# A transformer block on one core: seven products for eight in the second projection of the gated layer's first token block

## The chip, the core and the metric

The kernel runs on one core of a Trainium2 chip, in float32. The time is the device time of one execution, in microseconds (us), and the median of several runs is given. The engines that matter here are PE (matrix products; weights are loaded beside them, PEld), DVE (elementwise work and reductions, reads PE's result banks), ACT (activation functions and copies, reads the banks too), POOL (elementwise work on the on-chip memory only) and SP (issues transfers).

## The reference

A block of three layers over `x` of 2 x 1024 tokens x 256: self-attention with 16 heads of 64, cross-attention to 154 context tokens, and a gated layer, each on a layer norm of `x` and added to `x`. The gated layer, to which the change belongs:

```python
h = _layernorm(x, ln3_g, ln3_b)
p = h @ ff_w1 + ff_b1
a, gate = (p[..., :D_FF], p[..., D_FF:])              # D_FF = 1024
h = a * jax.nn.gelu(gate, approximate=False) @ ff_w2 + ff_b2
return h + x
```

Below, u is `a * gelu(gate)`, 1024 features for each token; the first projection is the product with `ff_w1`, the second the one with `ff_w2` (1024 x 256).

## The kernel before

The attention stages come first and fill most of the span. The gated layer runs in one loop at the end, over slots k = 0 to 63. Its tokens come in four blocks ("pairs") of 512, two of each batch element; a block is two halves j = 0, 1 of 256 tokens, and a half two tiles of 128. A unit n is one block and one slice f of 128 features (f = 0 to 7), and takes two slots: `gate_first(n)` in the even slot, `gate_second(n)` in the odd one. So block 0 is in slots 0 to 15, block 1 in 16 to 31, and so on.

**The first projection** makes, for a unit, the four 128 x 256 results (value and gate for both halves) from seven products for eight, a scheme after Strassen and Winograd: combined weights (`weight_sums`, made on POOL during cross-attention) and combined tokens (`token_sums`, four POOL operations for a block, called in slot 8 for block 1). DVE adds the parts (L1058, L1060, L1074, L1077, L1086), ACT applies the gate's function, and POOL multiplies value by gate: L1079 for half 1 at the end of `gate_second`, L1088 for half 0 in `gate_last`, which is called from the next unit's `gate_first`. These two write u.

**The second projection** of a block is queued in `sums` when its last unit is closed (slot 16 for block 0, 32 for block 1), and every slot takes two products of 256 columns, or one group of four products of 128 columns, from it.

- Block 0 is not in `FAST`: `sum_slot` (L1204) makes the plain product, eight products of 256 columns for each of four token tiles, 32 in all; DVE adds the result to `x` (L1214) and a transfer writes it out.
- Blocks 1 to 3 are in `FAST`: `fast_sum` (L1174) makes, for each half, seven groups g = 0 to 6 of four products of 128 columns. They read u itself (g=0, 1), mixes of u (s1, s2, s4, and one in the place of a21) and combined weights. DVE adds each group to its quarter of `x` (L1188); the first group is copied by ACT (L1182) and added to three quarters by POOL (L1183).

The mixes of u are `quick_tokens`: four POOL operations of 128 x 128 for each half and each pair of feature slices, queued in `combos` by `gate_last` when an odd f is closed. The combined weights of `ff_w2` are `quick_weights`: four POOL operations of 128 x 512 (L1136 to L1139). Both write a tile of the pool `pt`, tag `pT`, which `hold_quick` takes. That pool has two buffers: one holds the gated layer's weights (`wf`), the other the ring of cross-attention's turned probabilities, last read by PE in slot 5. `hold_quick` and the weights stand in slot k = 2 * NF + 2 = 18, and each slot takes two operations off `combos`.

**The order** on every engine is that of the program, written by hand: nothing reorders it, and an engine that waits holds up all that is behind. Within a slot stand, in this order: `gate_first` or `gate_second`, `token_sums` where due, the sums, the operations of `combos`, then `run_work`, which in odd slots takes a step from `side`, and an entry of `later` (L324 on POOL, the bias added to `x`). From slot 7 on, `side` holds the layer norm of the second batch element, which blocks 2 and 3 need: for two tiles a step, first statistics (DVE, L240, L241), a step later the variance and its root (POOL, L246, L250), a step later the offset (DVE, L256) and the normalization (POOL, L271, twice), and a step later four transposes on PE (L284). ACT moves the result to `hT`.

Of the kernel before, what the change touches and what calls it, by code (L numbers as in the profile page):

```python
# [10 lines left out]
ALU = mybir.AluOpType  # L11
# [7 lines left out]
def tile_transformer_block(ctx: ExitStack, tc: tile.TileContext, a: dict, out: bass.AP):  # L19
# [32 lines left out]
    NF = DF // P  # L52
# [45 lines left out]
    for n in names:  # L98
        k = n_of[n]
# [67 lines left out]
    for n in names[2:]:  # L167
        own = rows[row_of[n] - n_cols:row_of[n] - n_cols + n_of[n], :]
# [161 lines left out]
    def norm_beside(kind, b):  # L330

        after = {"sa": None, "ca": "sa", "ff": "ca"}[kind]
        stats, deviation, normalize, turn = norm_pieces(kind, b)
        n = 1 if narrow(kind, b) else 2
        lag = {}
        for fns, first in ((turn, 3), (stats, 0), (deviation, 1), (normalize, 2)):
            for i, fn in enumerate(fns):  # L340
                t = i if fns is stats else 2 * i + 1
                lag.setdefault(first + t // n, []).append((fn, fns is turn))
        for k in range(NT // n + 3):
            tiles = tile_order(kind)[k * n:(k + 1) * n]
            needs = [(after, b, half, t) for half in range(NQ) for t in tiles if after]

            def step(fns=lag[k]):
                slow.extend(fn for fn, _ in fns if fn in stats)
                done = [fn() for fn, _ in fns if fn not in stats]
                return next((fn for fn in done if fn), None)  # L350

            side.append((any(turns for _, turns in lag[k]), needs, step))
        if not narrow(kind, b):
            side.append((False, (), lambda: add_biases(kind, b)))
# [130 lines left out]
    def out_order(kind):  # L485

        return [t for t in tile_order("ff" if kind == "ca" else "ca") if t % 2 == 0]
# [75 lines left out]
    def run(piece):  # L563
        done = piece()
        if done is not None:
            (adds if getattr(done, "adds", False) else stores).append(done)

    def flush(queue):
        for fn in queue:
            fn()  # L570
        queue.clear()

    def run_work(n, n_side, bank=None, n_sum=0):

        while n > 0 and work:
            n -= work[0].banks
            run(work.pop(0))  # L580
        for _ in range(min(n_side, len(side))):
            needs_bank, needs, fn = side[0]
            if needs_bank and not bank and n <= 0 or not added.issuperset(needs):
                break
            if needs_bank and not bank:
                n -= 1
            spare["bank"] = bank or mm_tile
            run(fn)
            side.pop(0)
        if not spare["turned"]:  # L590
            flush(slow)
        for i in range(min(max(n, 0) + n_sum, len(outs))):
            spare["out"] = mm_tile if i < n else sum_tile
            run(outs.pop(0))

    def out_pieces(kind, b, half, tiles):
        outs.extend(lambda t=t: out_piece(kind, b, half, t) for t in tiles)
# [136 lines left out]
    CG = [(t, min(TG, NT - t)) for t in range(0, NT, TG)]  # L734
# [149 lines left out]
    def cross_regroup(c):  # L884

        ui, n = divmod(c - len(CG) - (1 if c > CA - 6 else 2), len(CG))
        if n != 0 or not 0 <= ui < NU:
            return
        for a2 in range(2):
            for a4 in range(P // KB):  # L890
                half, e = divmod(a4, 2)
                own = slice(a4 * KB, (a4 + 1) * KB)
                src = slice((2 * half + a2) * KB, (2 * half + a2 + 1) * KB)
                blocks = pTc["ring"][src, ui % 3, :2 * NM].rearrange("p (m e) j q -> p m e (j q)", e=2)
                nc.sync.dma_start(
                    out=pTc["pairs"][own, a2].rearrange("p m j q -> p m (j q)"), in_=blocks[:, :, e])
# [46 lines left out]
    def cross_drain(c):  # L943

        n = c - 2
        if 0 <= n < CA:
            cross_turn(n)

    def cross_weigh(c):

        ui, n = divmod(c - 2 * len(CG) - 1, len(CG))
        if n == 0 and 0 <= ui < NU:
            for part in (1, 0) if pools else (0, 1):
                run(lambda: cross_values(ui, part))
            flush(stores)


    NPR = B * 2
    BT = S // 4
    FU = NPR * NF  # L960
    wsum, wh, ub, psum, pools = {}, {}, {}, {}, {}
# [50 lines left out]
    def token_sums(pair):  # L1012

        b, t0 = divmod(pair * 2 * BT, S)
        h = hT["ff", b]
        own = [[h[:, c, t0 + j * BT:t0 + (j + 1) * BT] for j in range(2)] for c in range(NC)]
        t = pp_.tile([P, 3, BT], F32, tag="P", name=f"hs{pair}")
        nc.gpsimd.tensor_tensor(t[:, 0, :], own[0][1], own[0][0], ALU.subtract)
        nc.gpsimd.tensor_tensor(t[:, 1, :], own[1][1], t[:, 0, :], ALU.subtract)
        nc.gpsimd.tensor_tensor(own[0][1], own[1][1], own[0][1], ALU.subtract)  # L1020
        nc.gpsimd.tensor_tensor(t[:, 2, :], own[1][0], t[:, 1, :], ALU.subtract)
        wh[pair] = {
            1: own[0][0], 2: own[1][0], 3: own[1][1], 4: t[:, 2, :],
            5: t[:, 0, :], 6: t[:, 1, :], 7: own[0][1],
        }
# [55 lines left out]
    def gate_last(n):  # L1081
# [6 lines left out]
        nc.gpsimd.tensor_tensor(ub[pair][0][:, f, :], own[:, 0, :], own[:, 3, :], ALU.mult)  # L1088
        if pair in FAST and f % 2:
            for j in (1, 0) if pair == NPR - 1 else (0, 1):  # L1090
                engine = nc.vector if n == FU - 1 and j else nc.gpsimd
                combos.extend(((pair, j), fn) for fn in quick_tokens(pair, j, f // 2, engine))
        if f == NF - 1 and pair in FAST:
            order = [(j, g) for j in range(2) for g in range(7)]
# [5 lines left out]
                (lambda i=i, e=e: sum_slot(pair, i, e), 1) for i in range(2 * TF) for e in range(NF))  # L1100

    sums, summed, quick, combos, mixed = [], {}, {}, [], {}
    FAST = range(1, NPR)
    NHF = NF // 2

    def hold_quick():
# [34 lines left out]

    def quick_tokens(pair, j, c, engine=nc.gpsimd):

        u, own = ub[pair][j], quick["u", (2 * pair + j) % 4]
        (a11, a12), (a21, a22) = (
            [u[:, 2 * c + h, e * P:(e + 1) * P] for h in range(2)] for e in range(2))
        s1, s2, s4 = (own[:, i, c, :] for i in range(3))
        tt = engine.tensor_tensor
        mixed[pair, j] = mixed.get((pair, j), 0) + 1
        return [  # L1150
            lambda: tt(s1, a21, a22, ALU.add),
            lambda: tt(s2, s1, a11, ALU.subtract),
            lambda: tt(a21, a11, a21, ALU.subtract),
            lambda: tt(s4, a12, s2, ALU.subtract),
        ]

    def fast_sum(pair, j, g):
# [63 lines left out]
    with tc.manual_schedule():  # L1221
# [11 lines left out]
        own = [ps_s.tile([P, 2, HB], F32, tag="s", name=f"first_{r}") for r in range(2)]  # L1233
# [186 lines left out]
        for k in range(2 * FU):  # L1420
            c = CA + k
            if k == 0:
                run_work(0, 0, n_sum=2)
            flush(adds)
            (gate_second if k % 2 else gate_first)(k // 2)
            flush(stores)
            flush(lates)
            if k == 2 * len(CG) + 1:
                norm_beside("ff", B - 1)
            cross_drain(c)  # L1430
            if k % 2:
                cross_weigh(c - 1 if k == len(CG) + 2 else c)
            cross_regroup(c)
            if k == len(CG) + 2:
                out_pieces("ca", B - 1, NQ - 1, out_order("ca"))
            if k % (2 * NF) == NF and k < 2 * FU - 2 * NF:
                token_sums(k // (2 * NF) + 1)
            n_left = 2
            while n_left > 0 and sums:
                fn, n = sums.pop(0)  # L1440
                n_left -= n
                run(fn)
            flush(stores)
            if k == 2 * NF + 2:
                hold_quick()
                combos[:0] = [(None, fn) for fn in quick_weights()]
            for _ in range(min(2, len(combos))):
                combos.pop(0)[1]()
            run_work(0 if k == 1 else 1 + k % 2, k % 2)
            if later and (k <= len(CG) + 2 or k > 2 * NF):  # L1450
                if k <= len(CG) + 2 or k % 2:
                    later.pop(0)()
# [39 lines left out]
```

## Time and profile before

| | us |
|---|---|
| median of 3 runs | 1076.43 (1075.42 to 1077.2) |
| profiled execution, span | 1075.6 |
| busy PE / DVE / POOL / ACT | 1062.3 / 882.6 / 774.7 / 645.4 |
| slots k = 0 to 63 and the last sums | from 903.13 to the end |

The page gives the profiled execution's span and no other time for it. In a row of the timeline stand the start, the duration, the engine, the line of the kernel, the operation with what it writes and reads, its shape, how many follow each other, and in brackets an idle time before it with what ended it. A product in float32 leaves two records on PE. The tiles `quick` hold the combined weights and the mixes, `u` and `kT` the two halves of block 0's u, `own` a unit's parts, `pf` and `pq` the second projection's banks.

### The profile page before, as it was taken

How to read it: one execution, taken by the hardware profiler on the slowest of the kernel's cores; microseconds unless marked ns; L12 is line 12 of the kernel's file. 1: busy time of each engine (PE TensorE's matmuls, PEld its weight loads, DVE VectorE, ACT ScalarE, POOL GpSimd, SP SyncE). 2: the span in 40 equal slices, each digit the busy share in tenths (PEclk: the TensorE clock that was granted, in tenths of full speed). 3: DMA queues.
4: the chain of work that ended last, by engine and by line, in shares of the span. 5: the costliest groups of instructions: out<-in, count | busy, mean ns of one | idle time of the engine just before them, and what ended most of it. 6: DMA issues, size and time to landing. Idle time of an engine off the chain costs nothing.

```text
span 1075.6 us, 46812 instructions
## 1 busy us (share of the span) xinstructions
PE 1062.3 (99%) x19300; PEld 701.7 (65%) x19300; DVE 882.6 (82%) x1321; ACT 645.4 (60%) x2068; POOL 774.7 (72%) x1652
## 2 busy tenths in 40 slices
PE   8999999999999999999999999999999999999998
PEld 6556556566565565676655655566766677788998
DVE  5799999998989989999989898968877887655554
ACT  5766766677666666666777676665565564342231
POOL 2677777777777777777777777776666876499884
PEclk9999999999999999999999999999999999999999
DMA  3222122112111121111111101025776545000000
GB/s 91 65 74 48 44 48 53 43 43 50 31 43 31 33 51 34 38 43 24 44 24 34 43 24 38 16 57 138 173 171 169 124 107 113 17 5 16 21 10 30
DMA packets 104726, 60.84 MB, mean 57 GB/s; under 512 B 32378, under 2 KB 95298, under 8 KB 104514
## 3 DMA queue, kind: packets, MB, share of 16 engines
q1 hardware_dynamic: 103138, 57.07, 22.3%
q8 instruction: 152, 2.49, 1.0%
q10 hardware_dynamic: 1376, 0.79, 0.2%
q14 instruction: 60, 0.49, 0.2%
HBM read 27.91 MB, written 2.10 MB: 28 GB/s over the span
## 4 chain that ended last, share of the span: by engine, by line
PE 87%; DVE 3%; DMA 3%; POOL 3%; SPq 2%; issue 1%; ACT 1%; POOLq 0%; DVEq 0%; ACTq 0%
PE po L550 19%; PE s L498 18%; PE py_sa L472 5%; PE py_ca L472 5%; PE pv_sa L398 5%; PE pk_sa L367 4%; PE pq_sa L367 4%; PE pq_ca L367 4%; PE poc L914 4%; PE pb L1035 4%; PE pq L1174 3%; PE pa L1035 2%; PE sc L834 2%; PE pc L1035 2%; DMA st<-st 2%; SPq L519 2%
## 5 line engine op out<-in xcount | busy, mean ns | idle before, releaser
L622 POOL TENSOR_SCALAR p<-p,rd,ee 128x512 f32<-128x512 f32 x512 | 390.3, 768 | 91.3 <-DVE rd L612 88.2
L509 ACT ACTIVATE p<-s,st 128x512 f32<-128x512 f32 x512 | 345.0, 686 | 173.1 <-DVE st L684 170.4
L684 DVE TENSOR_REDUCE st<-s 128x2 f32<-128x1024 f32 x256 | 308.3, 1205 | 58.9 <-issue 18.2
L647 DVE STREAM_TRANSPOSE pT<-p 128x1024 f32<-128x1024 f32 x256 | 302.7, 1218 | 2.2 <-POOL p L622 2.1
L498 PE MATMUL s<-k_sa,q_sa 64*32 64x512 f32 x4096 | 252.9, 591 | 2.9 <-ACT p L509 2.2
L550 PE MATMUL po<-pT,v_sa 64*32 64x256 f32 x8192 | 237.1, 376 | 0.9 <-DVE pT L647 0.9
L550 PEld LDWEIGHTS po<-pT,v_sa 64*32 64x32 f32 x8192 | 172.6, 106 | 76.5 <-issue 30.6
L498 PEld LDWEIGHTS s<-k_sa,q_sa 64*32 64x32 f32 x4096 | 79.5, 106 | 102.9 <-issue 56.2
L851 ACT ACTIVATE p<-sc,neg 128x154 f32<-128x154 f32 x256 | 96.1, 403 | 79.9 <-DVE rden L859 76.3
L862 POOL TENSOR_SCALAR p<-p,rden 128x154 f32<-128x154 f32 x256 | 96.8, 399 | 52.8 <-DVE rden L859 52.6
L509 ACT ACTIVATION_READ_ACCUMULATOR p<-s,st 128x1 f32 x512 | 103.9, 203 | 0.0
L527 POOL TENSOR_TENSOR dd<-st 128x8 f32<-128x8 f32 x128 | 25.6, 200 | 73.8 <-DMA st<-st 70.8
L398 PEld LDWEIGHTS pv_sa<-sa_wv,hT_ln 64*128 64x128 f32 x1024 | 58.5, 188 | 14.2 <-issue 6.7
L398 PE MATMUL pv_sa<-sa_wv,hT_ln 64*128 64x128 f32 x1024 | 61.7, 275 | 0.0
L367 PE MATMUL pq_ca<-hT_ln,ca_wq 64*64 64x512 f32 (+1 forms) x544 | 59.9, 590 | 0.7 <-DMA ca_wq<-in_L_xattn_ca_wq_dram 0.5
L472 PE MATMUL py_ca<-ca_wo,o_ca 128*128 128x256 f32 x256 | 60.2, 383 | 0.0
L472 PE MATMUL py_sa<-sa_wo,o_sa 128*128 128x256 f32 x256 | 59.7, 385 | 0.3 <-ACT v_sa L407 0.3
L840 DVE TENSOR_REDUCE neg<-sc 128x6 f32<-128x924 f32 (+1 forms) x48 | 47.8, 995 | 14.8 <-PE sc L834 14.8
L472 PEld LDWEIGHTS py_sa<-sa_wo,o_sa 128*128 128x128 f32 x256 | 47.3, 190 | 18.4 <-issue 6.9
L367 PE MATMUL pq_sa<-hT_ln,sa_wq 64*32 64x512 f32 (+1 forms) x976 | 56.9, 586 | 0.0
L367 PE MATMUL pk_sa<-hT_ln,sa_wk 64*32 64x512 f32 x960 | 56.1, 590 | 0.3 <-ACT q_sa L382 0.3
L851 ACT ACTIVATION_READ_ACCUMULATOR p<-sc,neg 128x1 f32 x256 | 56.1, 219 | 0.0
(145 smaller groups left out, 1462.3 us busy)
## 6 DMA issues: line engine op xcount, KB each, us to landing
wf<-pT_ca SPq DMA_DIRECT2D x128, 128.0 KB, 2.4
st<-st SPq DMA_DIRECT2D x512, 1.0 KB, 1.8
v_sa<-v_sa SPq DMA_DIRECT2D x32, 256.0 KB, 4.1
sa_wq<-in_L_xattn_sa_wq_dram SPq DMA_DIRECT2D x32, 128.0 KB, 3.4
sa_wk<-in_L_xattn_sa_wk_dram SPq DMA_DIRECT2D x32, 128.0 KB, 3.3
sa_wv<-in_L_xattn_sa_wv_dram SPq DMA_DIRECT2D x32, 128.0 KB, 3.6
ca_wq<-in_L_xattn_ca_wq_dram SPq DMA_DIRECT2D x32, 128.0 KB, 3.4
wf<-in_L_xattn_ff_w_dram SPq DMA_DIRECT2D x12, 256.0 KB
```

The source lines that it names most:

```text
L367: nc.tensor.matmul(pq[r][f:f + m, at:at + n], lhsT=wt[own, c, f:f + m], rhs=h[own, c, t0:t0 + n], start=(c == 0), stop=(c == NH - 1), tile ...
L398: nc.tensor.matmul(pv[r][:, i * P:(i + 1) * P], lhsT=h[own, c, i * P:(i + 1) * P], rhs=wt[own, c, :], start=(c == 0), stop=(c == NH - 1), ...
L472: nc.tensor.matmul(py[:, e * D:(e + 1) * D], lhsT=o[:, i, (t + e) * P:(t + e + 1) * P], rhs=wo[kind][:, g * HP + i, :], start=(i == 0), st ...
L498: nc.tensor.matmul(sc[a4 * KB:(a4 + 1) * KB, j, :], lhsT=q[r, c:c + KB], rhs=k[r, h * HB:(h + 1) * HB], start=True, stop=True, tile_positi ...
L509: nc.scalar.activation(pr[:, j, :], sc[:, j, :], AF.Exp, bias=st[:, 0, 0, i, j:j + 1], accum_out=st[:, 0, 1, i, j:j + 1],)
L550: nc.tensor.matmul(po[a2][d:d + KB, :QH // 2], lhsT=v[r, t, e, d:d + KB], rhs=pT[r, d // DH * NK + n, :], start=(t == 0 and e == 0), stop= ...
L622: nc.gpsimd.tensor_scalar(pr[:, j, :], pr[:, j, :], own["rd"][:, c:c + 1], own["ee"][:, 0, c:c + 1], op0=ALU.mult, op1=ALU.mult,)
L647: nc.vector.transpose(halves[h][:, :, c:c + KB], slots[p]["p"][i].rearrange("p j (n k) -> p (j n) k", k=KB))
L684: nc.vector.tensor_reduce(st[:, 0, 0, i, :], sc[i], AX.X, ALU.max, negate=True)
L851: nc.scalar.activation(pr_[:, j, i, :T], sc[:, j, i * T:(i + 1) * T], AF.Exp, bias=neg[:, j, i:i + 1], accum_out=den[:, j, i:i + 1],)
L862: nc.gpsimd.tensor_scalar(pr_[:, j, i, :T], pr_[:, j, i, :T], rden[:, j, i:i + 1], 1.0, op0=ALU.mult, op1=ALU.mult,)
L1035: nc.tensor.matmul(into[:, :BT], lhsT=lhs, rhs=wh[pair][i], start=first, stop=True, skip_group_check=True)
```

## The change

Block 0 goes into `FAST`: its second projection is made by `fast_sum`, from mixes. Its mixes are queued from slot 4 on. `hold_quick` and the four weight operations go from slot 18 to slot 6 (2 * len(CG), where CG has three entries). No operation is taken off `combos` before slot 6, three a slot from 6 to 17, and two from 18 on. `quick_tokens` looks up its tile when an operation runs, not when it is queued, since the tile isn't there in slot 4. For block 0 there are 32 mixes more on POOL, 56 products of 128 columns for 32 of 256 on PE, and per half one copy on ACT, one addition on POOL and six on DVE, for four additions on DVE in all.

```diff
-    FAST = range(1, NPR)
+    FAST = range(NPR)
...
     def quick_tokens(pair, j, c, engine=nc.gpsimd):
-        u, own = ub[pair][j], quick["u", (2 * pair + j) % 4]
+        u = ub[pair][j]
...
-        s1, s2, s4 = (own[:, i, c, :] for i in range(3))
         tt = engine.tensor_tensor
+
+        def s(i):
+            return quick["u", (2 * pair + j) % 4][:, (0, 1, None, 2)[i - 1], c, :]
+
         mixed[pair, j] = mixed.get((pair, j), 0) + 1
         return [
-            lambda: tt(s1, a21, a22, ALU.add),
-            lambda: tt(s2, s1, a11, ALU.subtract),
+            lambda: tt(s(1), a21, a22, ALU.add),
+            lambda: tt(s(2), s(1), a11, ALU.subtract),
             lambda: tt(a21, a11, a21, ALU.subtract),
-            lambda: tt(s4, a12, s2, ALU.subtract),
+            lambda: tt(s(4), a12, s(2), ALU.subtract),
         ]
...
-            if k == 2 * NF + 2:
+            if k == 2 * len(CG):
                 hold_quick()
                 combos[:0] = [(None, fn) for fn in quick_weights()]
-            for _ in range(min(2, len(combos))):
+            n_mix = 0 if k < 2 * len(CG) else 3 if k < 2 * NF + 2 else 2
+            for _ in range(min(n_mix, len(combos))):
                 combos.pop(0)[1]()
```

The lines of the changed kernel lie one to four lower from here on (L1136 keeps its number, the mixes are L1154 to L1157, `fast_sum`'s product is L1177).

## The prediction

> **What bounds the kernel now.** I read the page first, then the stretches of the last stage (the windows view), then the chain of waits, and last the timelines of POOL and PE around the change. The page's engine row and the head of its chain:
>
> ```profile
> PE 1062.3 (99%) x19300; PEld 701.7 (65%) x19300; DVE 882.6 (82%) x1321; ACT 645.4 (60%) x2068; POOL 774.7 (72%) x1652
> PE 87%; DVE 3%; DMA 3%; POOL 3%; SPq 2%; issue 1%; ACT 1%; POOLq 0%; DVEq 0%; ACTq 0%
> ```
>
> PE is the bound over the whole span, so products saved on PE should come off the end, as long as nothing else becomes late. The windows view says where something might (after the stretch's length: busy us of PE, PEld, DVE, ACT, POOL, then PE's granted clock):
>
> ```profile
> 933.33:950.54 17.21, 16.12 (x76) 12.71 (x75) 13.07 (x38) 7.50 (x17) 15.95 (x27) 1.00 0.00 1
> 950.54:985.30 34.76, 34.76 (x166) 30.61 (x166) 16.82 (x41) 11.33 (x25) 32.68 (x53) 1.00 0.04 12
> ```
>
> In the gated layer's loop, the first stretch holds slots k=9 to 17, the second the rest up to k=31. From 933 to 951 us POOL is busy 15.95 of 17.21 us, and that is the one stretch where PE has gaps (16.12 of 17.21). The chain of waits and PE's timeline tie the two together:
>
> ```profile
> 945.18 1.09 POOL xn_ln L271 x2
> 953.78 0.86 PE pf L1204 x4
> 987.46 0.89 PE pq L1174 x8
> ```
> ```profile
> 941.21 0.70 PE L1035 MATMUL pb<-hT_ln,wf 128*128 128x256 f32 x2 [0.74 <-DVE own L1058]
> ...
> 950.59 1.03 PE L1204 MATMUL pf<-wf,u 128*128 128x256 f32 x4
> 951.45 0.60 PE L284 MATMUL ph_ln<-ident,xn_ln 128*128 128x128 f32 x4
> 951.88 0.60 PE L1035 MATMUL pa<-hT_ln,wf 128*128 128x256 f32 x2
> ```
>
> The chain itself runs through POOL's normalization of the second batch (L271) at 945 us: here POOL, not PE, already sets the pace for a moment. So I price PE's saving first and then POOL's load.
>
> **PE's saving.** A product leaves two records. Two old products of 256 columns (x4) take 0.86 us in the chain, 0.43 each, as the gate's products of the same shape do; four new ones of 128 columns (x8) take 0.89. Block 0 now has 16 slots of two, 13.8 us; it will have 14 slots of four, 12.5 us. The saving is 1.3 us, not an eighth more than that, because the narrow products run a little longer per column. By itself it would give 1075.6 - 1.3 = 1074.3 us of span.
>
> **POOL's added load.** POOL executes in order. Its timeline, from the first slot that changes (k=6) onward:
>
> ```profile
> 926.85 0.73 POOL L1088 TENSOR_TENSOR u<-own 128x256 f32<-128x256 f32 x1 [5.59 <-DVE own L1086]
> 931.22 0.72 POOL L1079 TENSOR_TENSOR kT<-own 128x256 f32<-128x256 f32 x1 [3.64 <-ACT own L1078]
> ...
> 934.01 0.73 POOL L1018 TENSOR_TENSOR hs<-hT_ln 128x256 f32<-128x256 f32 x1
> ...
> 936.87 0.73 POOL L1079 TENSOR_TENSOR kT<-own 128x256 f32<-128x256 f32 x1
> 937.67 0.19 POOL L246 TENSOR_SCALAR var_ln<-mv_ln 128x2 f32<-128x2 f32 x1
> 937.95 0.71 POOL L250 TENSOR_TENSOR rstd_ln<-var_ln,power 128x2 f32<-128x2 f32 x1
> 938.63 0.73 POOL L1088 TENSOR_TENSOR u<-own 128x256 f32<-128x256 f32 x1
> ...
> 941.15 1.09 POOL L271 TENSOR_SCALAR xn_ln<-x,rstd_ln,off_ln 128x256 f32<-128x256 f32 x2
> 942.21 0.73 POOL L1088 TENSOR_TENSOR u<-own 128x256 f32<-128x256 f32 x1
> ...
> 949.81 0.73 POOL L1088 TENSOR_TENSOR u<-own 128x256 f32<-128x256 f32 x1
> ...
> 954.97 1.27 POOL L1136 TENSOR_TENSOR quick<-wf 128x512 f32<-128x512 f32 x1
> 956.32 1.28 POOL L1137 TENSOR_TENSOR quick<-wf,quick 128x512 f32<-128x512 f32 x1
> 957.55 0.73 POOL L1079 TENSOR_TENSOR u<-own 128x256 f32<-128x256 f32 x1
> 958.23 1.28 POOL L1138 TENSOR_TENSOR quick<-wf 128x512 f32<-128x512 f32 x1
> 959.46 1.27 POOL L1139 TENSOR_TENSOR quick<-wf,quick 128x512 f32<-128x512 f32 x1
> 960.69 0.73 POOL L324 TENSOR_TENSOR x<-x,ff_b 128x256 f32<-128x256 f32 x1
> ...
> 976.52 0.46 POOL L1151 TENSOR_TENSOR quick<-u 128x128 f32<-128x128 f32 x1
> 977.06 0.45 POOL L1152 TENSOR_TENSOR quick<-quick,u 128x128 f32<-128x128 f32 x1
> 977.47 0.73 POOL L1079 TENSOR_TENSOR u<-own 128x256 f32<-128x256 f32 x1
> 978.15 0.46 POOL L1153 TENSOR_TENSOR u<-u 128x128 f32<-128x128 f32 x1
> 978.57 0.46 POOL L1154 TENSOR_TENSOR quick<-u,quick 128x128 f32<-128x128 f32 x1
> 978.98 0.73 POOL L324 TENSOR_TENSOR x<-x,ff_b 128x256 f32<-128x256 f32 x1
> ```
>
> I price each operation by start to next start in a run without idle time: a gate multiplication (L1079 or L1088) 957.55 to 958.23, 0.68; the four combined weights 954.97 to 957.55 and 958.23 to 960.69, 5.04 in all; the four token sums (L1018 to L1021) 934.01 to 936.87, 2.86; variance and root (L246, L250) 937.67 to 938.63, 0.96; a pair of normalizations (L271) 1.06; the four token mixes of one pair of columns 976.52 to 977.47 and 978.15 to 978.98, 1.78.
>
> The changed slots pop three operations each from k=6 on: the four weights in k=6 and 7, then mixes, 24 of them by k=15. The queue that decides runs from L1088 at 926.85 (gate of f=2) to the L1088 of f=7, the last half of u that block 0's second group of products (g=1, slot k=17) reads. In it stand:
>
> - 11 gate multiplications, 7.48
> - 4 combined weights, 5.04 (moved here from 954.97)
> - 4 token sums for block 1, 2.86
> - 24 mixes, 6 x 1.78 = 10.68 (new)
> - 4 times variance and root, 3.84, and 3 pairs of normalizations, 3.18
>
> The sum is 33.1 us, so that L1088 ends at 926.85 + 33.1 = 960.0 us if POOL never runs dry. Before, the same queue without weights and mixes is 17.4 us of work and ended at 950.5 (949.81 + 0.73): 6.3 us of idle time were in it. The change puts 15.7 us into 6.3 us of room, 9.4 too much.
>
> Does POOL run dry? At its first multiplications it has the three weights to do while L1079 of f=3 is not ready (931.22); 926.85 + 0.68 + 3.81 = 931.3 meets it. From there it only falls behind its suppliers. Nor does it wait for the buffer: the combined weights take that of the cross-attention ring, whose last reader on PE is done ahead of k=6.
>
> **What waits for POOL.** Three things, in order of program. First, DVE's offset (L256) waits for the root of the step before; in k=11 that root ends at about 942.0 instead of 938.65, and DVE's additions that free PE's banks stand behind it. That is the wait of 0.74 above grown to some 4 us (DVE has 1.1 us of statistics and two additions before it frees the bank, PE goes on at about 944.6). Second, PE's transposes (L284) in k=13 and 15 wait for L271: those pairs end at 948.1 and 954.1 on POOL, with PE ready at about 945.5 (two products after 944.6) and 951.6 (948.1 + 0.43 for the transposes, as 951.45 to 951.88, and seven products). Third, the products themselves: after the second transpose PE does 0.43, then k=16 with four products (1.73) and a group of sums (0.89), then k=17's three (1.30), and stands at g=1 at 958.5; the L1088 it needs ends at 960.0. These waits follow each other on one queue, so they don't add: the last, at 960.0, sets PE. Before, PE began that slot's sums at 950.59. PE is 9.4 us late there.
>
> **What comes after.** From k=17 PE has 13 slots x 0.89 = 11.6 for 15 x 0.86 = 12.9 us, so 1.3 come back. The four weights, 5.04 us, are gone from 955 to 961 us. Per two slots POOL then has two multiplications, four mixes and one bias addition (960.69's L324 takes as long as a multiplication), 1.37 + 1.78 + 0.68 = 3.83 us, against PE's 1.73 + 1.30 + 1.78 = 4.81. POOL gains on PE, so no more waits follow: the next groups (g=2, 3, 6) read mixes that POOL ends within 3.5 us of 960.0, and PE reaches g=2 at about 963. The two additions of the own product (L1183, 384 columns) I take at about 1 us each, between the 256 columns' 0.68 and the 512 columns' 1.25, and hidden by this margin; without it they would cost 2 us. ACT's two copies and DVE's twelve narrow additions for four wide ones lie on engines half idle in the third window (11.33 and 16.82 of 34.76): nothing. The transfers to the output stay four, SP's queue keeps its order: nothing.
>
> **Sum.** 1075.6 + 9.4 - 1.3 = 1083.7 us of span. The page gives no other time of that execution; 1075.6 lies 0.8 under the median of the runs, 1076.43. On the median I forecast 1084.5.
>
> The price of a mix depends on how one reads POOL. The rows' own durations overlap the next start by 0.04. [...] By spans the queue would be an estimated 33.8 us and the end 0.7 us later.
>
> Bounds: each mix at its shortest spacing (0.41) would take 0.9 us off the queue; spans add 0.7; a POOL that runs dry for a microsecond, and PE's refilling after three stops (0.1 each, the 0.70 for 0.59 above), add up to 1.3; the L1183 additions up to 2. So 1083.5 to 1088 with all of it against me, and 1083 to 1086.5 more likely.
>
> **Rivals.**
>
> *POOL has the room.* POOL is busy 72% of the span, and PE ran without a gap from 950.54 to 985.30 with POOL at 94%, so PE tolerates a POOL that lags. If the lag is absorbed, only the saving is left: 1076.4 - 1.3 = 1075.1, not slower. Against it: the tolerance there was for multiplications whose readers came a block later; here the transposes and g=1 read POOL's results one or two slots after they are made. The point from which it decides is a lag of some 3 us; I find 9.4. Chance 0.08.
>
> *The clock falls.* PE would stand for about 4.1 us, from 940.5 (941.21 less its wait) to 944.6, and 2.6 more up to 948.1. Both stretches quoted are granted 1.00, but the wait in them is of 0.74 us, so they can't show what a longer one does. If the clock halved, PE's slots k=14 to 16 (4.3 us for gate products and 0.89 for sums) would take twice as long; 2.5 us of that lies in the wait for the second transpose, so 2 to 4 us more: 1086.5 to 1088.5, say 1087.5. Chance 0.13.
>
> [...]
>
> *The forecast itself*, POOL's queue deciding at a full clock: chance 0.79.
>
> **How the numbers follow.** Two tenths of a per cent, 2.2 us, are about what can be told from no change. The forecast and the clock's rival are both slower by more; the room rival, at -1.3, is within it, and a little of the forecast too if most of the wait is hidden. Faster by over 0.2% would take a PE saving beyond 2.2 us, for which I see no row: 0.02. Same 0.08, slower 0.90. The range for 8 in 10 takes the forecast's own bounds from below with some room (1081.5) and reaches into the clock's rival (1088).
>
> **What would show it.** In the changed profile: the L1088 of f=7 ending near 960 with POOL busy without a break from 927; PE waiting on DVE's L1058 (about 4 us, k=13), on POOL's L271 (about 2.5 us twice) and on L1088 ahead of block 0's second group; that group starting near 960.0, and the slots from there on 0.89 for four products with no gap until 985. I am wrong if PE passes that group before 955, if the lateness grows again between 965 and 1000, or if the granted clock leaves 1.00.

## The result

Six runs of each kernel: 1085.36 us (1083.86 to 1086.29) against 1076.82 us (1075.42 to 1079.66) before, a ratio of 1.0077 with a 95% interval of 1.0064 to 1.0090. The change makes the kernel 8.5 us slower; the forecast was 8.1 us slower (1084.5 on 1076.43). The profiled execution took 1085.12 us, of which the span is 1083.0.

The kernels of this study reach the gated layer up to 3.2 us apart (900.57 to 903.79 us), although the code ahead of it is the same. So stage times below go from the first product of the loop (L1035) to the end of the span: 172.45 us before (903.13 to 1075.58), 180.89 after (902.15 to 1083.04). That is 8.4 us, all of the difference. Where an instruction of the two kernels is compared, its time since that first product is meant.

### The profile page after: what moved, and what is told of

Its sections match the earlier page's. It is cut to its first block, busy times and chain, and to the rows that moved or that the text cites. A ratio compares the mean times of both kernels' runs of the same rounds, so it can differ in the third digit from the quotient of the medians.

```text
span 1083.0 us, 46957 instructions
## 1 busy us (share of the span) xinstructions
PE 1064.4 (98%) x19348; PEld 706.9 (65%) x19348; DVE 885.1 (82%) x1329; ACT 645.6 (60%) x2070; POOL 792.0 (73%) x1686
## 4 chain that ended last, share of the span: by engine, by line
PE 80%; POOL 10%; DMA 3%; DVE 3%; issue 2%; SPq 2%; ACT 1%; POOLq 0%; DVEq 0%; ACTq 0%
PE po L550 19%; PE s L498 18%; PE py_sa L472 5%; PE pv_sa L398 5%; PE pk_sa L367 4%; PE pq_sa L367 4%; PE py_ca L472 4%; PE pq L1177 4%; PE pq_ca L367 3%; PE poc L914 3%; PE pb L1035 3%; PE sc L834 2%; DMA st<-st 2%; PE pa L1035 2%; PE pc L1035 2%
## 5 line engine op out<-in xcount | busy, mean ns | idle before, releaser
L367 PE MATMUL pq_sa<-hT_ln,sa_wq 64*32 64x512 f32 (+1 forms) x976 | 57.1, 586 | 0.0
```

The costliest lines, as they stand in the source:

```text
L367: nc.tensor.matmul(pq[r][f:f + m, at:at + n], lhsT=wt[own, c, f:f + m], rhs=h[own, c, t0:t0 + n], start=(c == 0), stop=(c == NH - 1), tile ...
```

## The profile after

From the page, the span, the engines' busy time and the head of the chain:

```profile
span 1083.0 us, 46957 instructions
PE 1064.4 (98%) x19348; PEld 706.9 (65%) x19348; DVE 885.1 (82%) x1329; ACT 645.6 (60%) x2070; POOL 792.0 (73%) x1686
PE 80%; POOL 10%; DMA 3%; DVE 3%; issue 2%; SPq 2%; ACT 1%; POOLq 0%; DVEq 0%; ACTq 0%
```

PE's busy time rose by 2.1 us although its work is less (part of it runs at half clock, below), POOL's by 17.3 us, and POOL's share of the chain went from 3% to 10%. On an average over the span the move is hardly visible (POOL 73% for 72%). The windows view shows where it is (busy us of PE, PEld, DVE, ACT, POOL, then the granted clock):

```profile
930.00:935.00 5.00, 5.00 (x25) 4.20 (x24) 4.08 (x12) 1.61 (x5) 4.84 (x8) 1.00 0.00 0
935.00:940.00 5.00, 4.35 (x19) 3.10 (x18) 2.30 (x7) 1.88 (x5) 4.97 (x10) 1.00 0.00 0
940.00:945.00 5.00, 1.43 (x3) 1.18 (x4) 2.88 (x9) 0.00 (x1) 4.71 (x10) 0.76 0.00 0
945.00:950.00 5.00, 3.80 (x11) 2.51 (x10) 1.95 (x8) 1.34 (x4) 4.84 (x11) 0.50 0.00 0
950.00:955.00 5.00, 5.00 (x20) 4.12 (x20) 2.52 (x7) 1.84 (x6) 4.76 (x11) 0.71 0.02 3
955.00:960.00 5.00, 4.33 (x30) 3.91 (x29) 2.25 (x6) 2.11 (x5) 4.84 (x9) 1.00 0.00 0
```

POOL has no idle time worth the name from 930 to 960, while PE falls to 1.43 of 5 us. POOL's timeline, from slot 6 to the multiplication that block 0's second group needs:

```profile
925.87 0.73 POOL L1088 TENSOR_TENSOR u<-own 128x256 f32<-128x256 f32 x1 [5.58 <-DVE own L1086]
926.57 1.26 POOL L1136 TENSOR_TENSOR quick<-wf 128x512 f32<-128x512 f32 x1
...
940.32 0.71 POOL L250 TENSOR_TENSOR rstd_ln<-var_ln,power 128x2 f32<-128x2 f32 x1
...
946.17 1.09 POOL L271 TENSOR_SCALAR xn_ln<-x,rstd_ln,off_ln 128x256 f32<-128x256 f32 x2
...
952.16 1.09 POOL L271 TENSOR_SCALAR xn_ln<-x,rstd_ln,off_ln 128x256 f32<-128x256 f32 x2
...
958.51 0.73 POOL L1088 TENSOR_TENSOR u<-own 128x256 f32<-128x256 f32 x1
```

The queue took 925.87 to 959.24, 33.4 us, without a bracket of idle time in between. The waits behind it, first that of DVE's offset, then those of PE:

```profile
941.07 0.67 DVE L256 SCALAR_TENSOR_TENSOR off_ln<-mv_ln,rstd_ln 128x2 f32<-128x2 f32 x1 [3.27 <-POOL rstd_ln L250]
```
```profile
943.57 1.22 PE L1035 MATMUL pb<-hT_ln,wf 128*128 128x256 f32 x2 [4.08 <-DVE own L1058]
944.59 1.06 PE L1035 MATMUL pc<-hT_ln,w1s 128*128 128x256 f32 x2
946.78 1.45 PE L284 MATMUL ph_ln<-ident,xn_ln 128*128 128x128 f32 x4 [1.13 <-POOL xn_ln L271]
948.01 1.06 PE L1035 MATMUL pa<-hT_ln,wf 128*128 128x256 f32 x2
...
953.44 0.60 PE L284 MATMUL ph_ln<-ident,xn_ln 128*128 128x128 f32 x4
...
957.80 0.83 PE L1177 MATMUL pq<-wf,u 128*128 128x128 f32 x6
959.29 0.49 PE L1177 MATMUL pq<-wf,u 128*128 128x128 f32 x2 [0.67 <-POOL u L1088]
959.62 0.60 PE L284 MATMUL ph_ln<-ident,xn_ln 128*128 128x128 f32 x4
...
996.28 0.83 PE L1177 MATMUL pq<-wf,u 128*128 128x128 f32 x6
997.50 0.49 PE L1177 MATMUL pq<-wf,u 128*128 128x128 f32 x2 [0.38 <-POOL u L1088]
997.82 0.60 PE L1035 MATMUL pa<-hT_ln,wf 128*128 128x256 f32 x2
```

The wait of 0.74 us before is now 4.08; the transposes of slot 13 wait for POOL's normalization; the second group of block 0 (six records, then two) waits for the multiplication that ends at 959.24. From 944 to 952 us products take 0.85 instead of 0.43 us: the granted clock there is 0.50. The transposes of slot 17 begin 57.47 us after the loop's first product (959.62 less 902.15) for 48.32 before (951.45 less 903.13): PE is 9.15 us late there. From those transposes to the end it takes 123.4 us for 124.1, so 0.7 us come back.

## The experiments

The theory is that POOL's queue between slots 6 and 17 gets 15.7 us of work for 6.3 us of room, and that DVE, the transposes and block 0's second group wait for it. The rivals are the narrow products, the earlier weights, and the clock. The stage column, from one profiled execution of each kernel, is comparable across all rows: the kernel before and the one with the weights alone both have 172.45, and the changed kernel and the two with filled waits lie within 0.03 of each other.

| | median | before, same chip | ratio (95%) | stage |
|---|---|---|---|---|
| weights alone | 1076.29 | 1075.76 | 1.0001 (0.9992 to 1.0010) | 172.5 |
| mixes unread | 1084.79 | 1075.76 | 1.0081 (1.0067 to 1.0095) | 181.1 |
| groups without mixes | 1074.83 | 1075.76 | 0.9997 (0.9988 to 1.0006) | 171.8 |
| first wait filled | 1085.11 | 1075.76 | 1.0089 (1.0075 to 1.0103) | 180.9 |
| both waits filled | 1084.76 | 1074.93 | 1.0090 (1.0076 to 1.0104) | 180.9 |
| weights and mixes early | 1081.56 | 1074.93 | 1.0054 (1.0040 to 1.0067) | 177.7 |
| room on POOL | 1075.74 | 1074.93 | 1.0005 (0.9996 to 1.0014) | 172.4 |
| the same, plain block 0 | 1075.15 | 1074.93 | 1.0000 (0.9991 to 1.0009) | 172.1 |
| and order, later groups | 1075.32 | 1076.02 | 0.9991 (0.9982 to 1.0000) | 171.6 |
| and order, plain block 0 | 1076.06 | 1076.02 | 0.9999 (0.9990 to 1.0008) | 172.1 |
| half the normalizations on POOL | 1077.57 | 1076.17 | 1.0013 (1.0003 to 1.0022) | 174.0 |
| all of them on POOL | 1079.51 | 1076.17 | 1.0031 (1.0020 to 1.0043) | 175.8 |

**Which part costs.** Three kernels take the change apart. Weights alone:

```diff
-    FAST = range(NPR)
+    FAST = range(1, NPR)
```

> Only the combined weights go to slot 6; block 0 keeps its plain products and has no mixes. Theory (POOL's queue between slots 6 and 17 gets 15.7 us where it has 6.3 us of room): 5.0 us fit into the room, POOL's idle times before its first multiplications shrink, and PE goes on as before: 1076.8, within 1 us. Rival (the earlier writing of the weights and of their tile is itself what holds things up): 3 us or more above 1076.8.

Nothing changed, in time or in PE's waits, although POOL is nearly full from 926 to 933 us; windows and waits of this run:

```profile
925.87:933.33 7.46, 7.46 (x36) 6.51 (x35) 5.49 (x14) 1.36 (x3) 7.02 (x7) 1.00 0.00 1
```
```profile
PE pb L1035 <- DVE own L1058: 0.7, 1, 0.7
PE ph_ln L284 <- POOL xn_ln L271: 0.2, 1, 0.2
```

The 5.0 us lie in POOL's idle time. Next, the mixes made but not read, with plain products:

```diff
-    FAST = range(NPR)
+    FAST, MIXED = range(1, NPR), range(NPR)
...
-        if pair in FAST and f % 2:
+        if pair in MIXED and f % 2:
...
-            lambda: tt(a21, a11, a21, ALU.subtract),
+            lambda: tt(a21 if pair in FAST else s(4), a11, a21, ALU.subtract),
```

> As the changed kernel, but block 0's second projection is made by the plain products from u; its mixes are made by POOL and read by nobody (the one that would overwrite u goes to another place in the tile). Theory (POOL's queue): PE is held up by the same transposes, 8.2 us late at slot 17, and nothing is saved afterwards: 1085.0, between 1083.5 and 1086.5. Rival (the narrow products, their small additions to x or the reading of the mixes cost the time): 1076.8, within 1 us.

The whole loss is there without one narrow product in block 0 (1.0081, and 8.7 us in the stage where 8.2 was expected), and PE waits on the same two things:

```profile
PE pb L1035 <- DVE own L1058: 4.3, 1, 4.3
PE ph_ln L284 <- POOL xn_ln L271: 2.3, 2, 2.1
```

Last, the groups with no mixes:

```diff
-        if pair in FAST and f % 2:
+        if pair and f % 2:
...
-        lhs = (a11, a12, own[:, 1], a21, a22, own[:, 0], own[:, 2])[g]
+        lhs = (a11, a12, own[:, 1], a21, a22, own[:, 0], own[:, 2])[g] if pair else (
+            a11, a12, a11, a21, a22, a12, a22)[g]
```

> As the changed kernel, but block 0's mixes are left out and its groups of products read u itself in their places (so block 0's output is another one): the narrow products alone, with the weights in slot 6. Theory (POOL's queue): the saving of PE is bare, 1.3 us: 1075.5, between 1074.5 and 1076.5. Rival (the narrow products cost the time): 1080 or more.

The stage is 0.7 us shorter than with the weights alone (171.8 for 172.5), half of the 1.3 expected; in whole runs that is less than the interval can tell. The other half went to a wait for POOL in block 1, which comes below. So the mixes on POOL cost the time, and neither the weights nor the products do. Nor does the added work on POOL make DVE slower: its additions (L1058) take 0.42 us each from 925 to 960 us in both kernels. DVE only waits.

**Is it the clock?** Transposes that nobody reads fill PE's waits in slot 13:

```diff
+        if n == 6:
+            idle = sum_tile('idle')
+            for _ in range(32):
+                nc.tensor.transpose(idle[:, :P], ident, ident)
         product(n, 7, pb, False)
```

> As the changed kernel, with 32 transposes of 128 columns that nobody reads put on PE in slot 13, ahead of the product that waits for DVE, so that PE works through most of its 4.1 us wait and its clock should stay full. Theory (POOL's queue alone sets the end, the half clock runs inside waits): 1085.4, within 0.7 us. Rival (part of the loss is the clock): 1 to 3 us less, 1082.4 to 1084.4.

The time is that of the changed kernel, as expected, but the test was not clean: the clock fell all the same, after a wait of 2.08 us for the transposes. PE's row and the window behind it:

```profile
946.05 1.44 PE L284 MATMUL ph_ln<-ident,xn_ln 128*128 128x128 f32 x4 [2.08 <-POOL xn_ln L271]
```
```profile
945.00:950.00 5.00, 3.88 (x11) 3.05 (x12) 1.66 (x6) 1.29 (x3) 5.00 (x11) 0.53 0.00 0
```

So 36 transposes there, and 20 more behind the products of slot 13:

```diff
         product(n, 3, pc, False)
+        if n == 6:
+            for _ in range(20):
+                nc.tensor.transpose(idle[:, :P], ident, ident)
```

> As the changed kernel with transposes that nobody reads in both long waits of slot 13, 36 ahead of the product that waits for DVE and 20 ahead of the transposes that wait for POOL, so that the granted clock stays at 1.00 through them (with 32 in the first wait alone it fell to 0.5 after the second). Theory (POOL's queue sets the end, the half clock runs inside waits): 8.3 us above the kernel before, within 0.8. Rival (part of the loss is the clock): 1 to 3 us less than that.

```profile
940.00:945.00 5.00, 4.83 (x41) 4.40 (x40) 3.56 (x10) 0.51 (x1) 4.69 (x10) 1.00 0.00 0
945.00:950.00 5.00, 4.61 (x26) 3.50 (x24) 3.02 (x10) 1.77 (x4) 5.00 (x11) 1.00 0.00 0
```
```profile
951.72 0.33 PE L284 MATMUL ph_ln<-ident,xn_ln 128*128 128x128 f32 x1 [1.89 <-POOL xn_ln L271]
952.25 0.55 PE L284 MATMUL ph_ln<-ident,xn_ln 128*128 128x128 f32 x3 [0.21 <-POOL xn_ln L271]
```

Now the clock is 1.00 throughout, and the stage is again 180.9 us. The transposes of slot 15, which PE reached at half clock when POOL was just done, now wait 1.89 and 0.21 us for POOL. So the half clock costs nothing here: the time that it takes is time in which PE would have waited for POOL. In whole runs this kernel is 9.7 us above the kernel before, more than the 7.5 to 9.1 expected; its interval overlaps that of the changed kernel, and the stage shows no such extra.

**Giving POOL room.** If the queue is the cause, work taken out of it, or put into idle time ahead of it, must come off the end. First the weights in slot 5 and eight mixes in slot 6:

```diff
-            if k == 2 * len(CG):
+            if k == 2 * len(CG) - 1:
...
-            n_mix = 0 if k < 2 * len(CG) else 3 if k < 2 * NF + 2 else 2
+            n_mix = {5: 4, 6: 8}.get(k, 0 if k < 5 else 3 if k < 2 * NF + 2 else 2)
```

> As the changed kernel, but the four weights stand in slot 5 and the first eight mixes in slot 6, so that POOL does them in the idle times it has before 930 us. Theory (POOL's queue): 4.8 us more stand ahead of the multiplication of f=3, about 1 us of it is lost to new idle time behind, so the end is 3.8 us earlier than the changed kernel's: 4.5 us above the kernel before, between 3.5 and 6. Rival (the loss hangs on the mixes' number, not on where they stand): 8.5 above.

Nothing is taken off POOL, only put elsewhere, and 3.2 us of the 8.4 go (177.7 for 180.9). I expected 3.8. The whole runs are 5.8 us above the kernel before by the ratio, inside the range but near its upper end, and 6.6 by the medians, outside it. Then, besides, block 1's token sums in slot 4 and the normalization on ACT:

```diff
-            if k % (2 * NF) == NF and k < 2 * FU - 2 * NF:
+            if k == 4 or k > NF and k % (2 * NF) == NF and k < 2 * FU - 2 * NF:
...
-                if not narrow(kind, b) or first and i == 1:
+                if not narrow(kind, b) and (kind, b) != ("ff", B - 1) or first and i == 1:
```

> As the one before, and besides the token sums of block 1 go from slot 8 to slot 4 (2.9 us of POOL into its idle time) and the second batch element's normalization goes from POOL to ACT (3.2 us off the queue). Theory (POOL's queue): the queue then holds about 16.4 us of work from 932.8 on and ends at 949.2, where it ended before; nothing of the lateness is left and the saving of PE shows: 1.3 us below the kernel before, between 2.5 below and 0.5 above. Rival (ACT's normalizations hold up the gate's functions behind them, or DVE's offsets wait on): 2 us or more above.

The loss is gone, with all mixes still on POOL, but the gain isn't there. PE's waits in it say why:

```profile
PE pa L1035 <- ACT own L1054: 1.3, 1, 1.3
PE pq L1177 <- POOL u L1088: 0.4, 1, 0.4
```

ACT's copy (L1054) stands behind the normalizations, which wait for DVE's offset and so for POOL's root (0.37 us at 936.79, ahead of PE's wait of 1.28): part of the rival came true. The same room with plain products:

> The same room on POOL as in the one before (weights in slot 5, token sums of block 1 in slot 4, normalization on ACT), but block 0 keeps its plain products and has no mixes. Theory: PE's two waits of the kernel before, 0.74 and 0.21 us, go: 0.9 us below the kernel before; the difference to the one with block 0's groups is their own worth, 1.3 us at most. Rival (the room by itself does nothing): equal to the kernel before.

That is 0.3 us less in the stage than the kernel before, not 0.9 (whole runs can't tell either from nothing): here too PE waits on ACT, 0.57 us. Two more edits aim at the two waits, the norm's step ahead of the mixes and block 0's groups from slot 18 on:

```diff
-            while n_left > 0 and sums:
+            while n_left > 0 and sums and k >= 2 * NF + 2:
...
+            if 2 * len(CG) <= k < 2 * NF + 2:
+                run_work(1 + k % 2, k % 2)
             n_mix = {5: 4, 6: 8}.get(k, 0 if k < 5 else 3 if k < 2 * NF + 2 else 2)
...
-            run_work(0 if k == 1 else 1 + k % 2, k % 2)
+            if not 2 * len(CG) <= k < 2 * NF + 2:
+                run_work(0 if k == 1 else 1 + k % 2, k % 2)
```

> The kernel with room on POOL and block 0's groups (weights in slot 5, eight mixes in slot 6, token sums in slot 4, normalization on ACT), with two more edits: in slots 6 to 17 the norm's step stands ahead of the mixes, so that the root, and with it ACT's normalization, comes 1.3 us sooner; and block 0's groups start in slot 18, so that slots 30 and 31 are not short and block 1's second group doesn't reach POOL's product too soon. Theory (each wait of PE left in the stage is one of those two, 1.54 + 0.40 and 0.54 us, and the groups by themselves save 1.3): 2.3 us below the kernel before, between 1.3 and 3 below. Rival (the groups are worth nothing on the chip): equal to the kernel before or above.

> The same without block 0's groups and mixes: plain products from slot 16 on, the room on POOL, and the norm's step ahead of the mixes, of which there are none before slot 18. Theory: the root waits for the gate's multiplication ahead of it as it did with the room alone, so PE keeps waits of about 0.8 and 0.4 us on ACT: 0.3 us below the kernel before, within 0.7; block 0's groups are then worth 2 us here. Rival (what is gained above comes from the room and not from the groups): the same time as with the groups.

With the groups the stage is 171.6, 0.8 below the kernel before; with plain products (and no wait for slot 18) 172.1. The first is the shortest stage of the study, but the interval of its ratio ends at 1.0000, so whether it beats the kernel before stays open. Of the 2.3 us expected 0.8 came. The plain kernel is 0.3 below the kernel before, as expected, but that makes the groups worth 0.5 us in the stage and not 2, and whole runs can't tell the two kernels apart. The wait in block 1 is gone, but 0.8 us of waits on ACT's copy are left:

```profile
PE pa L1035 <- ACT own L1054: 0.8, 2, 0.6
```

POOL's root is not what holds ACT up ahead of these two: it ends at 936.42 and 941.05, and DVE's offset starts at 937.36 and 941.28 without a wait for it. By the program's order ACT does the gate's function (L1078), the two normalizations and then the copy; in the kernel before a normalization on ACT (L274) takes 0.59 us and that function 0.51. That ACT goes through them without a pause is my estimate. To take these waits away, half or all of the normalization went back to POOL (for half: `((kind, b) != ("ff", B - 1) or i == 1)` in the condition; for all, the condition as in the changed kernel):

> As the kernel with all four edits and block 0's groups (weights in slot 5, token sums in slot 4, norm's step ahead of the mixes, groups from slot 18), but of each pair of normalizations one goes to ACT and one stays on POOL. Theory (the waits of PE that are left there, 0.87, 0.46 and 0.40 us, are ACT's copy standing behind two normalizations of 0.5 us): they shrink by half or more, 0.5 to 1.2 us less in the stage, so 1.3 to 2 us below the kernel before. Rival (POOL is full again with four more normalizations of 0.53 us): above the kernel with all on ACT.

> The same with both normalizations back on POOL. Theory (POOL's queue): 3.2 us more stand in its queue before the last transposes, of which the order of the norm's step ahead of the mixes and the later groups hide a part; PE waits on POOL's normalizations again, 0 to 3 us above the kernel with the split. Rival (ACT's copy was the only wait left): below the split.

The first expectation failed and its rival held: the waits on ACT went, and larger ones on POOL came. The second held, 1.9 us above the split in the stage. PE's waits with half and with all of it on POOL:

```profile
PE ph_ln L284 <- POOL xn_ln L271: 3.0, 3, 1.5
```
```profile
PE ph_ln L284 <- POOL xn_ln L271: 4.0, 6, 1.6
PE pb L1035 <- DVE own L1058: 0.5, 1, 0.5
```

From none to half, and from half to all, three normalizations of 0.53 us come onto POOL ahead of the last transposes that wait, 1.6 us of work each time. The stage goes from 171.6 to 174.0 to 175.8. POOL is full in these slots even after all the room that was made (no idle time in brackets from 935.54 to 967 us with half, from 933.93 to 967 with all of it): what is put there comes out at the end, 2.4 and 1.9 us for 1.6. Why it is more than the work, these runs don't show.

## Why the prediction was right

**The saving of PE: the mis-sized term.** Forecast 1.3 us, measured 0.7 (123.4 for 124.1 us after the transposes of slot 17; 171.8 for 172.5 in the experiment with bare groups). The price of a slot was right: a group of four takes 0.89. What failed is "no more waits follow": block 0's groups end two slots early, slots 30 and 31 carry none, and PE comes to block 1's second group before POOL has multiplied its last slice (0.38 in brackets). That group takes 1.54 us to the next product's start (996.28 to 997.82) for the usual 0.89, 0.65 more: about all that is missing. With the groups from slot 18 that wait is gone. I had compared POOL's rate with PE's over slots that have a group, not over the two that have none.

**POOL's queue.** Forecast 33.1 us from the first multiplication, measured 33.4, and never dry. Start-to-start prices from other places in the trace carried over to 0.3 us in 33. Counted from the loop's first product, L1088 of f=7 ends 9.7 us later than before (57.1 for 47.4 us); forecast 9.4.

**The waits.** DVE's offset, the first transposes and the second group wait as forecast, and the waits don't add. Three details differ. Only the last of the group's four products reads the last slice, so three run ahead of the wait, and PE is 9.15 us late behind it although POOL is 9.7 late. The transposes of slot 13 wait 1.13 us, not 2.6: the two products ahead of them run at half clock, rows of 1.22 and 1.06 us (with rows of 0.70 and 0.59, in the first test of the clock, the wait is 2.08), and the first of the four transposes needs only the first of the two normalizations, done 0.5 us sooner. And those of slot 15 don't wait at all: PE, at half clock, arrives at 953.44, when POOL's normalization (952.16, 1.09) is just done.

**The clock.** This rival came true in its condition and failed in its price. That a wait of some 4 us could halve the clock was not shown by any run ahead of the forecast; the changed kernel shows it. The granted clock fell to 0.50, and slots 14 and 15 took 5.4 us (948.01 to 953.44) for 3.0. These 2.4 us went into the wait for POOL that the forecast put at 2.5 us. It had seen that cover, but let slot 16 run at half clock as well; a product was back at 0.43 us by 953.0 (granted 1.00 from 953 to 954). So two of the signs that I had named for being wrong came up: the granted clock left 1.00, and the lateness grew again, by the 0.65 us at 997. The first changed nothing at the end; the forecast had put 2 to 4 us on it, so that its number held in spite of the half clock is luck. The second is the mis-sized term.

**Room on POOL as a rival** fell: the lag that POOL may have is set by who reads it next, and mixes that nobody reads cost 8.7 us of the stage.

**The sum.** +9.4 - 1.3 = 8.1 forecast, +9.15 - 0.7 = 8.4 in the traces, 8.5 in the medians. The lateness was taken 0.25 too long and the saving 0.6 too large, and the two errors work against each other; the first is small because POOL ends 0.3 us later than forecast while three products run ahead of the wait. That the total came so close is in part luck. The 0.8 from span to median, too, compares two different things: within one execution the device time is 1.7 to 1.9 us above the span in the kernel before, as the experiments ran it, and 2.1 to 2.2 in the changed one (1085.12 for 1083.0). It changes the difference by 0.3 to 0.4 us.

## What to carry to other kernels

A trade of PE work for work on a helper engine is priced in the stage in which it lands, by that engine's queue written out in program order and against its idle time there, not by its share of the span: POOL's 72% over the span was 93% from 933 to 951 us. Ask of each result of that engine how soon it is read; a lag that is free for one reader stops the next one cold. And when a stage gets shorter, look at who now arrives too early: here half of PE's saving went into a wait in the next block.

## What was not expected of the hardware

PE's clock halved in four of the kernels, and among the profiled executions the mean granted clock is below 1.00 in these alone (0.995 in the changed one, 0.997 with mixes that nobody reads, 0.997 with the first wait filled, 0.998 with the weights and mixes early). In the changed one it fell over a wait of 4.08 us (granted 0.50 from 944 to 952). With mixes that nobody reads the two products behind a wait of 4.35 were still at full clock (rows of 0.70 and 0.62 us), and the transposes behind a further wait of 2.06 took 1.44 us for 0.60 (window 945 to 950 granted 0.65). With the weights and mixes early it fell around a single wait of 3.5 (records of up to 0.63 us for 0.38), and with the first wait filled after waits of 0.61 and 2.08 with two products between (window 945 to 950 granted 0.53). With transposes that nobody reads in both places the longest wait of PE in the stage was 1.9 us and the clock stayed at 1.00. How long a wait has to be, and how separate waits are weighed together, these runs don't show.
